# Mixing the end of layer 0 into layer 1's first projections

## The chip, the cores and the metric

The kernel runs on one core of one Trainium2 chip. A core has five engines that work at the same time and wait for one another by semaphores: PE (TensorE, matmuls, with its weight loads shown as PEld), DVE (VectorE), ACT (ScalarE), POOL (GpSimd) and SP (SyncE, which here only starts DMA transfers). Matmul results land in PSUM, which has eight banks; everything else is held in SBUF or in the chip's HBM. The metric is the device time of one execution in microseconds (us), lower is better.

## The reference

Two layers, each x + s * silu(f), where s is an attention and f a feed-forward network (FFN), both of the same layer-normalized input. The input is 4 batches of 512 tokens of 512 numbers.

```python
x  = L0_attn_x                                   # (4, 512, 512)
xn = _layernorm(x, axis=-1)
s  = _L0_attn_ref(xn, ...)    # softmax attention, 32 heads of 16, 8 key/value heads
g  = _silu(_L0_ffn_ref(xn, ...))   # Hadamard-mixed, gated: silu(x Wg) * (x Wu), then W_down
x  = x + s * g
xn = _layernorm(x, axis=-1)
s  = _L1_attn_ref(xn, ...)    # gated delta rule: q, k, v by projection, causal conv of 4, silu; 6 heads of 64
g  = _silu(_L1_ffn_ref(xn, ...))   # relu MLP with sign(weights), 512 -> 2048 -> 512
x  = x + s * g
```

In layer 1 the projections come first: q, k and v are x W, then a convolution over four time steps, then silu; a gate x Wg and two small columns (beta and the decay) are computed beside them. Then a scan over the tokens, which the kernel does in tiles of 128 tokens with a triangular solve.

## The kernel before

The program is written in program order, one helper after the other, and a scheduler at build time lays down each engine's order: it takes what is earliest in program order and, by its own estimate of durations, ready. On the chip each engine then runs its list strictly in that order and waits where an operand isn't there.

**Layer 0** is a loop over units `u`. A unit of attention is a quarter of the heads' work on 128 tokens: with 4 batches and 8 groups of heads there are `NU` = 256 units, 8 in each set of (batch, group). In unit `u` the loop emits:

- `maxima(u)`, L399 and L400: two score matmuls into the PSUM tile `sc` (one buffer of two banks), and a DVE reduction of it to the row maxima `nmx`;
- `exps(u - 11)`, L420 and L422: the transposed scores into `st` (one buffer of two banks) and exp on ACT into `pe`;
- after every eighth unit `max_rows` (L405 to L411), which folds the maxima into the queries, and, 11 units later, `values` (L430 to L452): 32 small matmuls, a copy to `os`, a round trip through HBM that turns the sums into reciprocals (`sum_d`, `rc`, `rec_d`, `sm`, with a DVE reciprocal at L440), the product on POOL (L446, `oT`) and four DMAs into `oTc`;
- two half pieces of the FFN, `ffn(v, 0)` and `ffn(v, 1)`, of the piece `v = u - 16`. A batch has 64 pieces: in the first 32 `gate_up` (L313, 4 matmuls a half, weights from `wS` by DMA, drained by ACT and DVE at L319 to L324), in the last 32 `down` (L331, 1 matmul call a half, two instructions; the PSUM tile `y` collects 16 halves and is drained at L334 and L335 into `g`).

For the batch before, `layer_sum` (L462 to L467: out projection of the attention, times `g`, POOL adds x, stored to `x1_d`) and `norm1` (L61 to L69 statistics with an ACT square root, L73, four transposes at L476, ACT copy, stored to `xn1_d`) are emitted at fixed units of the next batch. The last batch has no next one. There the loop stops at unit 269, `end_of_layer0` emits the FFN pieces 254 and 255, the four sums and the four norms, and layer 1 follows.

**Layer 1's projections** are a list of steps with weights: `projections(0)` fills `steps` with `gate1` for the last block (L741; weight 4.0), `decays`, nine times `project` (L689; 8 matmul instructions; L695 on ACT, three times L697 on DVE, L701 on ACT, L702 on DVE; weight 3.4), `to_tokens` one projection later (L713, four transposes, a square and, at L727, a DVE reduction; 0.45), two more `gate1` (3.6 each) and `norms`. The weights come by `load_wp` (L598) into three buffers of `wp`, on SP's queue between the other DMAs. PSUM for all of these is `bank()`, three buffers of one bank, which take the place of `sc` and `st` once attention has ended. Before, the steps are emitted in one go after `end_of_layer0`.

After them `l0.close()` gives back layer 0's SBUF and PSUM. Into that space go, among others, the small constants of layer 1 (L846 to L856, the loads on ACT's queue; L856 multiplies `drow` by `osc` on DVE), the copies `xsh` and `xsl` of the input (L871, L873), and the FFN of layer 1, `up1` (L913) and `down1` (L927), whose pieces are spread between the steps of what follows. The next stage, `within` (L959 to L987), begins the scan's tiles.

Of the kernel before, what the change touches and what calls it, by code (L numbers as in the profile page):

```python
# [19 lines left out]
NB, SEQ, DM = 4, 512, 512  # L20
NT = NB * SEQ // P
TB = SEQ // P
# [11 lines left out]
def kernel(ctx: ExitStack, tc: tile.TileContext, i: dict, out: bass.AP):  # L34
# [66 lines left out]
    if True:  # L101
# [164 lines left out]
        def fold_down(a):  # L266
            ph = misc()
            nc.tensor.matmul(ph, hmat, wdn[:, a, :], start=True, stop=True)
            nc.vector.scalar_tensor_tensor(wdn[:, a, :], ph, cdn[:, a : a + 1], drow, ALU.mult, ALU.mult)
# [67 lines left out]
        def ffn(u, part):  # L337
            b, r = u // 64, u % 64
            if r < 32:
                gate_up(b, r // 2, r % 2, part)  # L340
            else:
                down(b, (r - 32) // 8, 2 * (r % 8) + part)
# [7 lines left out]

        sets = [(b, g) for b in range(NB) for g in range(HG)]
        NU, LAG, LATE = 8 * len(sets), 11, 16
        qds, qTs, nmxs, qms, pes = {}, {}, {}, {}, {}

        def queries(b, v, jj):
# [123 lines left out]
        piece, zp = [0], []  # L481
# [18 lines left out]
        for n in range(FF // P):  # L500
            u = LATE + 2 * n - 4
# [3 lines left out]
        for q in range(NI):  # L505
            early.setdefault(q, []).append(lambda q=q: mix_down(q))

        for u in range(NU + LATE):
            b, r = u // 64, u % 64
            v = u - LATE  # L510
            piece[0] = max(v, 0)
            if v == 32:
                top.close()
                zp.append(l0.enter_context(tc.tile_pool(name="zp", bufs=2, side="right")))
            if 0 < u - LAG <= NU and (u - LAG) % 8 == 0:
                values((u - LAG) // 8 - 1)
            if u < NU:
                maxima(u)
            if 0 <= u - LAG < NU:
                exps(u - LAG)  # L520
            for f in early.get(u, ()):
                f()
            if v >= 0:
                ffn(v, 0)
                ffn(v, 1)
            if u % 8 == 7 and u < NU:
                max_rows(u // 8)
            if u % 32 in (22, 23) and u + 10 < NU:
                queries((u + 10) // 64, (u + 10) % 64 // 32, u % 32 - 22)
            if u % 8 == 0 and u + 8 < NU:  # L530
                set_queries(u // 8 + 1)
            if 16 <= v < 16 + NI:
                fold_down(v - 16)
            if 0 < b < NB and r in (18, 19, 20, 21):
                layer_sum(b - 1, r - 18)
            if 0 < b < NB and r in (25, 26, 28, 29):
                norm1(b - 1, (25, 26, 28, 29).index(r))
            if b + 1 < NB:
                if r == 34:
                    load_x(b + 1)  # L540
                if r in (43, 44, 45, 46):
                    stats0(b + 1, r - 43)
                if r == 49:
                    norm0(b + 1)
                if r == 52:
                    keys_values(b + 1)
            if u == NU + LAG + 2:
                break

        def end_of_layer0():  # L550
            for v in range(NU + LAG + 3 - LATE, NU):
                piece[0] = v
                ffn(v, 0)
                ffn(v, 1)
            for t in range(TB):
                layer_sum(NB - 1, t)
            for t in range(TB):
                norm1(NB - 1, t)

    att.close()  # L560

# [219 lines left out]
    steps = []  # L781
# [48 lines left out]
            add(0.0, *between.pop(0))  # L830

    projections(0)
    end_of_layer0()
    for _, f, args in steps:
        f(*args)
    steps.clear()
    l0.close()

# [475 lines left out]
    n = 0  # L1314
    for count, pinned, l in parts:
        total, done, first = sum(x[0] for x in l), 0.0, n
# [54 lines left out]
```

## Time and profile before

| | us |
|---|---|
| three runs, median (lowest, highest) | 1551.44 (1547.99, 1556.83) |
| the profiled execution | 1545.31 |
| its span, first to last instruction | 1543.5 |
| PE busy / DVE / ACT / POOL | 1452.9 / 1061.2 / 693.9 / 360.1 |
| last `maxima` (L399) starts | 761.6 |
| last `values` (L430) starts | 791.3 |
| last FFN matmul of layer 0 (L331) ends | 800.7 |
| first step of layer 1 (L741) starts | 801.6 |
| last `gate1` of the first projections (L741) ends | 875.2 |

How to read it: the page gives the busy time of each engine over the span, and the span in forty slices. A timeline row is start, length, engine, line, operation, the tiles written and read, how many instructions, and in square brackets how long the engine stood idle before the row and what ended that idle time. "x20" after a matmul row is twenty instructions back to back. Busy time of PE is that of pipelined matmuls, so the useful number is where it is not busy. A row's waiting engine isn't always to blame: the wait has a releaser, which may itself have waited.

### The profile page before, as it was taken

The numbers are of one execution on the slowest core, as the hardware profiler recorded it, in microseconds if no ns is written. First come the engines' busy times: TensorE is split into PE (matmuls) and PEld (weight loads), VectorE is DVE, ScalarE is ACT, GpSimd is POOL, SyncE is SP. The second block draws the span as 40 slices with busy tenths as digits, with TensorE's granted clock in tenths as the row PEclk, the third lists the DMA queues.
The fourth block names the chain that finished last, engine by engine and source line by source line (L and its number), as shares of the span: only waits on it lengthen the run. The fifth ranks groups of instructions, "written<-read, shape, count | busy, mean of one in ns | idle before, by whom it ended". The sixth has DMA issues, their size and how long they took to land.

```text
span 1543.5 us, 22781 instructions
## 1 busy us (share of the span) xinstructions
PE 1452.9 (94%) x8144; PEld 870.2 (56%) x8144; DVE 1061.2 (69%) x1890; ACT 693.9 (45%) x1009; POOL 360.1 (23%) x350
## 2 busy tenths in 40 slices
PE   6999999999999999999997999999999999988896
PEld 3466533555345543465343566876578756865674
DVE  6899755765566655665417679579956896588675
ACT  4654554665456654575433435224332434232132
POOL 1012100321013310222003421243204422244012
PEclk9999999999999999999998999999999999999798
DMA  8956300564026620364025343425452545224323
GB/s 281 345 184 207 139 24 22 190 226 138 25 67 211 221 84 23 120 228 143 19 80 166 94 120 104 118 83 157 132 146 55 151 125 151 70 83 145 100 79 106
DMA packets 201753, 199.14 MB, mean 129 GB/s; under 512 B 65480, under 2 KB 153000, under 8 KB 200744
## 3 DMA queue, kind: packets, MB, share of 16 engines
q1 hardware_dynamic: 198888, 196.55, 40.5%
q10 hardware_dynamic: 2752, 1.14, 0.3%
q8 instruction: 64, 1.05, 0.3%
q14 instruction: 49, 0.40, 0.1%
HBM read 146.84 MB, written 46.19 MB: 125 GB/s over the span
## 4 chain that ended last, share of the span: by engine, by line
PE 63%; DVE 23%; DMA 5%; issue 3%; POOL 2%; ACT 2%; SPq 2%; ACTq 0%; DVEq 0%; POOLq 0%
PE y L331 15%; PE mm L313 12%; PE y L927 4%; PE ph L913 4%; PE sc L399 4%; DVE UT L1022 3%; DVE sx L1018 3%; DVE yc L697 2%; PE pu L741 2%; DVE nmx L400 2%; PE mm L430 2%; PE pu L1120 2%; PE pu L1144 2%; PE pu L982 2%; PE pu L969 1%
## 5 line engine op out<-in xcount | busy, mean ns | idle before, releaser
L400 DVE TENSOR_REDUCE nmx<-sc 128x2 f32<-128x1024 f32 x256 | 312.3, 1220 | 163.5 <-PE st L420 150.4
L422 ACT ACTIVATE pe<-st 128x1024 f16<-128x1024 f32 x256 | 262.6, 1026 | 147.7 <-PE st L420 146.6
L331 PE MATMUL y<-wdn,hT 128*128 128x512 f32 x512 | 252.5, 617 | 3.2 <-DVE g L335 1.7
L313 PE MATMUL mm<-xr,wc 128*128 128x512 f32 x768 | 206.4, 410 | 0.0
L313 PEld LDWEIGHTS mm<-xr,wc 128*128 128x128 f32 x768 | 137.3, 189 | 48.6 <-issue 21.7
L324 POOL TENSOR_TENSOR hT<-hT,th 128x512 f32<-128x512 f32 x64 | 84.1, 1314 | 330.9 <-ACT hT L323 299.9
L331 PEld LDWEIGHTS y<-wdn,hT 128*128 128x128 f32 x512 | 87.1, 189 | 97.3 <-issue 89.7
L689 PE MATMUL pu<-xn1T,wp 128*128 128x512 f32 x288 | 132.9, 605 | 0.0
L898 ACT ACTIVATE sg<-sw 128x512 fp32r<-128x512 f32 x128 | 79.7, 625 | 113.8 <-issue 51.4
L913 PE MATMUL ph<-xsh,sg 128*128 128x512 f32 x256 | 114.3, 446 | 2.8 <-ACT sg L898 2.8
L399 PE MATMUL sc<-kT,qT 32*128 32x512 f16 x512 | 103.3, 384 | 6.5 <-DVE nmx L400 5.9
L446 POOL TENSOR_TENSOR oT<-os,sm 128x512 f16<-128x512 f32 x32 | 41.2, 1287 | 280.5 <-DMA sm<-rec_d 231.0
L913 PE MATMUL ph<-xsl,sg 128*128 128x512 f32 x256 | 103.5, 404 | 0.0
L420 PE MATMUL st<-qm,kT 32*128 32x512 f16 x512 | 101.4, 385 | 1.6 <-ACT pe L422 1.6
L399 PEld LDWEIGHTS <-qT 32*128 32x128 f16 x512 | 26.3, 91 | 132.4 <-issue 128.2
L927 PE MATMUL y<-sg,hsh 128*128 128x512 f32 x256 | 84.0, 439 | 9.2 <-DVE hsh L871 5.7
L918 ACT ACTIVATE hT<-ph,upsc 128x512 f32<-128x512 f32 x64 | 43.7, 683 | 102.5 <-PE ph L913 102.3
L689 PEld LDWEIGHTS pu<-xn1T,wp 128*128 128x128 f32 x288 | 54.7, 195 | 57.3 <-issue 55.8
L313 PE MATMUL mm<-xr,fo 128*128 128x512 f32 x256 | 74.1, 423 | 0.9 <-DVE fo L244 0.9
L927 PE MATMUL y<-sg,hsl 128*128 128x512 f32 x256 | 73.6, 402 | 0.0
L319 ACT ACTIVATE th<-mm,hwg 128x512 f32<-128x512 f32 x64 | 44.0, 688 | 57.7 <-PE mm L313 57.7
L1022 DVE TENSOR_TENSOR UT<-UT,sx 96x31 f32<-96x31 f32 (+31 forms) x155 | 67.2, 434 | 3.3
(285 smaller groups left out, 2426.0 us busy)
## 6 DMA issues: line engine op xcount, KB each, us to landing
wc<-wS SPq DMA_DIRECT2D x96, 512.0 KB
wS<-fo SPq DMA_DIRECT2D x16, 1024.0 KB
sw<-in_upT SPq DMA_DIRECT2D x64, 256.0 KB
sw<-in_downT SPq DMA_DIRECT2D x64, 256.0 KB
sm<-rec_d SPq DMA_DIRECT2D x128, 64.0 KB
raw<-in_w_gateT SPq DMA_DIRECT2D x8, 512.0 KB
hT<-in_w_downT SPq DMA_DIRECT2D x16, 256.0 KB
raw<-in_w_upT SPq DMA_DIRECT2D x8, 512.0 KB
```

Source lines behind the costliest of these rows:

```text
L313: nc.tensor.matmul(pgs[m], wcs[b, c, m][:, h, k, :], xrs[b][:, k, :], start=(k + h == 0), stop=(k == KC - 1 and h == 1))
L324: nc.gpsimd.tensor_tensor(hT, hT, ths[b, c], ALU.mult)
L331: nc.tensor.matmul(ys[t], hTs[b, c][:, ts(t, P)], wdn[:, c, :], start=(c == 0), stop=(c == NI - 1))
L399: nc.tensor.matmul(sc[:, j, :], qTs[n][rows, ts(t, P)], kTs[b, g // 4][rows, :], start=True, stop=True)
L400: nc.vector.tensor_reduce(nmxs[n][:, t, 2 * pr : 2 * pr + 2], sc, AX.X, ALU.max, negate=True)
L420: nc.tensor.matmul(st[:, j, :], kTs[b, g // 4][rows, ts(k, P)], qms[n][rows, :], start=True, stop=True)
L422: nc.scalar.activation(pes[u], st, AF.Exp)
L689: nc.tensor.matmul(pp, wps[b, n][:, k, 0:P], xn1Ts[b][:, k, :], start=(k == 0), stop=(k == KC - 1))
L898: tc.keep_in_program_order(nc.scalar.activation(sgs[b, c, m], raws[b, c, m], AF.Sign))
L913: ins = nc.tensor.matmul(ph, sgs[b, c, 0][:, ts(k, P)], xss[b][n][:, k, :], start=(k + n == 0), stop=(k == KC - 1 and n == 1))
L927: ins = nc.tensor.matmul(yss[b][t], hss[b, c][n][:, ts(t, P)], sgs[b, c, 1], start=(c + n == 0), stop=(c == NI - 1 and n == 1))
L1022: nc.vector.tensor_tensor(U[:, 0 : j + 1, j + 1 :], U[:, 0 : j + 1, j + 1 :], x, ALU.add)
```

## The change

Two things are changed.

In layer 0's loop, the FFN no longer runs at two half pieces a unit to the end. `halves(u)` counts the half pieces emitted before unit `u`: up to unit 212 it is 2 (u - 16) as before, from there on it grows by 3 halves in 2 units. Unit 212 is the 21st of the last batch, and the rate holds through the rest of that batch's `gate_up` and the first part of its `down`. The loop now ends with unit 267, that of the last `values`, when 476 of the 512 halves are out.

The other 36 halves, the four `layer_sum` and the four `norm1` of the last batch go into a list `rest`. The steps of `projections(0)` are then emitted as before, and after each step as many items of `rest` as keep the share of `rest` at 1.5 times the share of the steps' weight. `end_of_layer0` is gone. What each helper computes, and its tiles, stay as they are.

```diff
         sets = [(b, g) for b in range(NB) for g in range(HG)]
-        NU, LAG, LATE = 8 * len(sets), 11, 16
+        NU, LAG, LATE, SLOW = 8 * len(sets), 11, 16, 212
+
+        def halves(u):
+
+            return 2 * (min(max(u, LATE), SLOW) - LATE) + (3 * max(u - SLOW, 0) + 1) // 2
+
...
-        for u in range(NU + LATE):
+        for u in range(NU + LAG + 1):
             b, r = u // 64, u % 64
-            v = u - LATE
+            v = halves(u) // 2 if u >= LATE else u - LATE
             piece[0] = max(v, 0)
...
-            if v >= 0:
-                ffn(v, 0)
-                ffn(v, 1)
+            for h in range(halves(u), halves(u + 1)):
+                ffn(h // 2, h % 2)
...
-            if u == NU + LAG + 2:
-                break
-
-        def end_of_layer0():
-            for v in range(NU + LAG + 3 - LATE, NU):
-                piece[0] = v
-                ffn(v, 0)
-                ffn(v, 1)
-            for t in range(TB):
-                layer_sum(NB - 1, t)
-            for t in range(TB):
-                norm1(NB - 1, t)
+
+        def last_half(h):
+            piece[0] = h // 2
+            ffn(h // 2, h % 2)
+
+        rest = [(last_half, h) for h in range(halves(NU + LAG + 1), 2 * NU)]
+        rest += [(f, NB - 1, t) for f in (layer_sum, norm1) for t in range(TB)]
...
     projections(0)
-    end_of_layer0()
-    for _, f, args in steps:
+
+    total, done, n = sum(x[0] for x in steps), 0.0, 0
+    for w, f, args in steps:
         f(*args)
+        done += w
+        while n < len(rest) and n < 1.5 * len(rest) * done / total:
+            rest[n][0](*rest[n][1:])
+            n += 1
     steps.clear()
     l0.close()
```

## The prediction

> **What bounds the kernel now.** First the page: busy shares and the forty slices.
>
> ```profile
> PE 1452.9 (94%) x8144; PEld 870.2 (56%) x8144; DVE 1061.2 (69%) x1890; ACT 693.9 (45%) x1009; POOL 360.1 (23%) x350
> ...
> PE   6999999999999999999997999999999999988896
> ```
>
> TensorE is busy for 94% of the span, so moved work can gain only where it stands still. Slices are 38.6 us; the only dip inside the kernel is the 7 in the 22nd (811 to 849 us), where layer 0 hands over to layer 1. Next, the busy time by stretches there (columns: stretch, length, busy us and count of PE, weight loads, DVE, ACT, POOL, then granted clock, DMA share, GB/s).
>
> ```profile
> 800.00:810.00 10.00, 10.00 (x50) 6.58 (x49) 4.98 (x19) 2.50 (x6) 1.26 (x1) 1.00 0.37 111
> 810.00:820.00 10.00, 6.11 (x27) 3.10 (x26) 9.12 (x25) 1.44 (x3) 4.49 (x4) 1.00 0.36 118
> 820.00:830.00 10.00, 7.43 (x25) 3.50 (x24) 9.94 (x18) 5.76 (x8) 0.00 (x0) 0.83 0.53 163
> 830.00:840.00 10.00, 7.94 (x26) 3.71 (x24) 5.17 (x8) 4.97 (x9) 4.18 (x8) 1.00 0.71 199
> 840.00:850.00 10.00, 7.12 (x18) 3.79 (x19) 4.72 (x9) 2.56 (x5) 2.95 (x5) 0.66 0.53 162
> 850.00:860.00 10.00, 8.57 (x28) 4.07 (x27) 8.79 (x12) 4.88 (x8) 5.33 (x6) 1.00 0.21 61
> ```
>
> From 800 to 875, where the first projections end, PE is busy for 61.13 of 75 us: **13.87 us idle**. From 810 to 830 DVE is full instead; from 830 to 850 nothing is. The timeline tells which waits these are.
>
> ```profile
> 791.86 8.85 PE L331 MATMUL y<-wdn,hT 128*128 128x512 f32 x20
> ...
> 819.38 0.66 PE L713 MATMUL pu<-identf,yc 128*128 128x128 f32 x4 [3.52 <-DVE yc L702]
> 819.88 5.29 PE L689 MATMUL pu<-xn1T,wp 128*128 128x512 f32 x8
> 827.06 1.11 PE L476 MATMUL mm<-identf,xn 128*128 128x128 f32 x8 [1.89 <-DVE xn L73]
> ...
> 842.88 1.11 PE L713 MATMUL pu<-identf,yc 128*128 128x128 f32 x4 [4.95 <-DVE yc L702]
> 843.79 5.36 PE L689 MATMUL pu<-xn1T,wp 128*128 128x512 f32 x8
> ```
>
> The last FFN matmuls end at 800.7; from then on no filler is left. At 819 the transposes of the first projected block wait for DVE, which ran layer 0's sums and statistics first. At 843 they wait again, and DVE itself stood at one instruction:
>
> ```profile
> 841.74 0.49 DVE L856 TENSOR_SCALAR drow<-drow,osc 128x512 f32<-128x512 f32 x1 [4.13 <-DMA osc<-in_output_scale]
> ```
>
> The chain of waits names what is before it: the last store of normalized rows (2.73 us), whose end frees layer 0's memory, then 5.07 us for a load of one number. Eight projection matmuls take 3.60 us elsewhere, but 5.29 and 5.36 after these two idles, and four transposes 1.11 instead of 0.60: the slower clock cost 1.69 + 1.76 + 0.51 = **3.96 us**. With the idle, 17.8 us are lost. The smaller idles are 0.38, 1.89 and 0.68 (sums and normalization) and 0.16 + 1.26 + 1.03 = 2.45 (later projections).
>
> The Trainium skill, "TensorE: Matmul & The Clock Gate", Part 1, states that the clock falls to half once an activity window of about 3.4 us was idle and needs a busy one to recover. Here idles of 3.52 and 4.95 us were followed by mean clocks of 0.83 and 0.66, and the idles of 1.89 and less by none. By that rule a stall cut to half of 4.95 us costs no clock; were the clock's loss to shrink in proportion instead, 1.1 us of it would remain and the sum below would be 1.1 us smaller.
>
> **Part 1: attention runs ahead from unit 212.** Before, each unit carries two half pieces of FFN; after, one and a half. Before unit 267 the halves issued fall from 502 to 475, 27 fewer. No matmul is added or removed. Four down matmuls in the steady state take 1.91 us, so 27 halves are 25.8 us: the last set's value product moves from 791.3 to about 765.5, and 36 halves stay for the mix instead of the 10 in the x20 row.
>
> The cost is cover. A unit's two score pairs take 0.32 us of PE, a gate half 2.06 / 2 = 1.03, a down half 0.96. The score bank is single, and its shortest turn seen is 1.69 us:
>
> ```profile
> 719.80 0.25 DVE L440 RECIPROCAL rc<-rc 128x16 f32<-128x16 f32 x1 [1.57 <-DMA rc<-sum_d]
> 719.97 0.63 DVE L320 SCALAR_TENSOR_TENSOR th<-th,mm 128x512 f32<-128x512 f32 x1
> 720.51 1.21 DVE L400 TENSOR_REDUCE nmx<-sc 128x2 f32<-128x1024 f32 x1
> 722.20 1.22 DVE L400 TENSOR_REDUCE nmx<-sc 128x2 f32<-128x1024 f32 x1 [0.48 <-PE st L420]
> ```
>
> A unit with two halves lasts 2.38 us and hides it; one with a single half lasts 1.35 and doesn't. The mean, 1.5 x 1.03 + 0.32 + about 0.15 for the value products, is 2.0 us, above 1.69. If the built order pulls the next half forward, nothing is lost. If it keeps strictly to the program, 18 gate units lose 0.34, three down units 0.41 and six units after the last score 0.35 (exp's own turn, 48.25 to 49.88, is 1.63, against 0.32 + 0.96): 6.1 + 1.2 + 2.1 = 9.4 us. The order isn't strict: between 45 and 52 us eight gate matmuls are cut into groups of 1, 5 and 2 around attention matmuls. I take 2 us, nearest to the 724 to 768 stretch, where PE lost 0.57 of 44 us (1.3%, so 1.4 of the 110 us that 55 units of 2.0 last), and a little for the thinner cover; both ends, 0 and 9.4, stay for the range. The weight loads of the gate halves (512 KB each on SP) come no denser per PE time than before.
>
> **Part 2: 36 halves, four sums and four norms mixed into the projections.** Step weights total 46.15, and 44 items go out at 1.43 per unit of weight: six after the gate step, then about five per projection; halves end after projection 5, sums and norms after projection 6. So:
>
> - The 3.52 us wait and its 1.69 of clock go. For projections 0 to 5 DVE has 3.6 us of work each (three at 0.74, 0.69, 0.68), PE has 3.44 + 0.44 + 5 x 0.89 = 8.3 us. The transposes come after about 4.4 us of halves and a 3.4 us projection, their chain takes about 5. Saved: 5.2 us.
> - The sums and norms still come in a burst, now over projections 5 to 8: DVE has 2.6 (sums), 3.2 (statistics), 2.4 (root, four normalizations), 3.5 (L871 and L873) and three projections (10.8), 22.5 us; PE has 3.5 + 1.8 + 3 x 3.9 + 3.7 = 20.7. POOL's four adds at 1.17 pass three squares at 1.04 (L726), 7.8 us and no bound. Of 2.95 us idle, half stays. Saved: 1.5 (0 to 2.95; DVE's surplus could add 2).
> - L856 still stands in DVE's queue behind a 5.07 us load that starts when the norm store ends. What waits behind it is the conv chain of a projection. Cover is now projection 8 and two gate steps (3.4 + 3.7 + 3.8), which need little of DVE but are limited by three banks. Half of 4.95 stays; 2.5 us of idle is nearer to the 1.89 that cost no clock than to the 3.52 that did, so the 2.27 goes. Saved: 4.7 (0 to 7.2).
> - The 2.45 us of late projections stay.
>
> Saved together 11.4 us. Moved DMAs: four 256 KB stores of x1 and four of xn1 on SP, past the weight loads of projections 7 and 8; their reader is batch 3's projection, hundreds of us later, so they cost nothing unless they hold SP's queue.
>
> **New costs.** The gate step needs a 1 MB xn1T and a weight load, issued when the value product ends; before, 9.6 us of FFN and sums covered them exactly. Now the halves behind it do, if the order places enough: 0 to 4 us (the weight load waited 3.9 us on SP for wba), I take 0.5, since PE waits for no load in the listing of waits. About twenty more switches between FFN and projections cost 0 to 2 us (a first L913 behind L689 took 0.64 against 0.23), I take 0.5, as most switch between alike matmuls.
>
> The Trainium skill, same page, Part 2, "Step-by-step", says that only weight loads are pulled ahead and matmuls stay in program order. It speaks against the change: a half queued behind a waiting transpose fills nothing. Rows agree, as at 819.38 the eight matmuls queued behind ran only 0.5 us after the wait ended. By the rule any misjudged order costs its full wait, by the sum above only what the built order left uncovered.
>
> **The sum:** 11.4 - 2 - 0.5 - 0.5 = 8.4 us. The profiled execution took 1545.31 us (span 1543.5); minus 8.4 it is 1536.9, a factor of 0.9946. On the median of 1551.44 that is 1543.
>
> **Rivals.**
> 1. *Everything covered.* All 17.8 us go at 1 us of cost: 1545.31 - 16.8, on the median 1534.6. For it: FFN filler exceeds the idle twice over. Against: halves end by projection 5, before the burst and L856.
> 2. *The stalls come back.* Burst and L856 stall in full with their clock, the gain of the first wait is eaten by the burst's longer DVE queue, and 3 us of new cost remain: 0 to +3, 1553. For it: L856 isn't touched. It holds if PE idles as much after the mix as before.
> 3. *Attention's score bank becomes the bound, slower.* Units 212 to 267 run strictly in order: 9.4 us, and the seven waits for rc, which stand in DVE's queue ahead of the reductions, cost their 1.57 each, because no slack is left: 11.0. Sum 20.4 + 1 - 11.4 = +10, 1561.5. For it: single halves last less than the bank's turn. Against: the cut groups. It decides from 12 us lost there.
>
> **How the numbers follow.** Forecast 0.47 (own range 1538 to 1548), rival 1 0.15, rival 2 0.20, rival 3 0.18. About 0.5% (7.8 us, so 1543.7 and 1559.2) can be told from no change. Faster: rival 1 and 0.6 of the forecast, 0.43. Slower: most of rival 3, 0.17. Same: the rest, 0.40. The range 1534 to 1559 leaves out half of rival 1 and over half of rival 3, together under 0.2.
>
> **What would show it.** Last L399 near 742 instead of 761.6, and PE over 97% busy from 650 to 766. No L713 wait above 1 us while L331 still runs; the first L741 without a DMA wait. L856 again waiting for osc, with a PE wait under 3.4 us and no clock below 1.0. Projections ending near 866 instead of 875. Idle at L399 or L420 of 10 us and more would make the prediction wrong, as would a gap at the first gate step.

## The result, and the profile after

The changed kernel takes **1555.36 us** (median of 14 runs, 1550.98 to 1559.83) and the kernel before 1550.54 us (14 runs beside it). The ratio is 1.0037, interval 1.0021 to 1.0052: slower by 0.4%, where 0.5% faster was forecast. On a second chip the unchanged pair gave 1.0066 (1.0043 to 1.0089). The profiled execution of the changed kernel took 1559.80 us (span 1558.1), that of the kernel before 1545.31 (1543.5). These two lie 14.5 us apart and the medians 4.8, so the profiles overstate the loss; they say where it lies in one execution, the ratios how large it is.

Line numbers behind L350 are 5 or 6 higher than before: the score matmul is now L405, its reduction L406, the exp's matmul L426, the division L446, the gate step's L741 and the projection's L689 are unchanged, drow is L861, the sign L903, the first matmul of layer 1's FFN L918. In the experiments' own traces the lines stand up to 19 higher; the names of the tiles are the same.

First the page: busy shares, TensorE's forty slices and its clock.

```profile
PE 1460.6 (94%) x8144; PEld 877.1 (56%) x8144; DVE 1065.0 (68%) x1890; ACT 693.0 (44%) x1007; POOL 360.9 (23%) x350
...
PE   6999999999999999999989899999999999998796
...
PEclk9999999999999999999999999999999999999798
```

The 7 of the 22nd slice is gone, and instead the 21st (779 to 818 us) and the 23rd (857 to 896 us) show an 8. PE's busy time grew by 7.7 us with the same 8144 matmuls, for the most part by the slower clock (6.8 us in the ledger below). The busy time by stretches of 25 us shows the places (columns as before: stretch, length, busy us and count of PE, weight loads, DVE, ACT, POOL, then granted clock, DMA share, GB/s).

```profile
675.00:700.00 25.00, 22.13 (x111) 13.09 (x111) 14.81 (x18) 13.65 (x18) 5.14 (x4) 0.86 0.57 185
...
775.00:800.00 25.00, 19.99 (x79) 9.03 (x79) 1.63 (x5) 6.66 (x9) 2.48 (x7) 0.86 0.36 95
800.00:825.00 25.00, 25.00 (x75) 12.28 (x75) 13.62 (x38) 5.74 (x12) 1.27 (x1) 1.00 0.20 58
825.00:850.00 25.00, 25.00 (x67) 11.34 (x66) 10.38 (x15) 5.76 (x10) 1.04 (x1) 1.00 0.11 31
...
875.00:900.00 25.00, 19.40 (x115) 13.91 (x114) 12.30 (x17) 6.68 (x13) 18.68 (x25) 0.92 0.62 195
```

From 800 to 850, where the kernel before stood most, PE is busy for 50.00 of 50 us: the mixing does what it says. The loss is ahead of it and behind it. The ledger below cuts both traces at the same events. Idle is the time in which no matmul's record runs; the clock's loss is half the length of each window that the profile marks with half clock.

| stage, to its last event | length before, after | idle before, after | lost to clock before, after |
|---|---|---|---|
| attention: reduction of unit 208 to last exp | 155.0, 148.1 | 1.68, 9.14 | 0, 3.41 |
| handover: to the first gate matmul (L741) | 12.0, 12.5 | 0.00, 5.01 | 0, 3.14 |
| projections: to the last L689 | 61.6, 67.4 | 12.84, 0.98 | 5.12, 0.27 |
| two gate steps: to their last L741 | 11.7, 15.3 | 1.03, 2.61 | 0, 1.71 |
| next: to the next batch's first L741 | 23.6, 33.7 | 1.38, 5.23 | 0, 3.41 |
| sum | 263.9, 277.0 | 16.93, 22.97 | 5.12, 11.94 |

Idle and clock together grew by 6.04 + 6.82 = 12.86 us of the 13.1 by which the stretch grew: the ledger closes to 0.3 us, so nearly all of the loss is waiting and slower clock. Behind it both traces run alike (14.5 us apart at the first gate matmul of the next batch, 14.6 at the end). Three new waits are the largest parts of it; the timelines show them (start, duration, engine, line, operation, in brackets the idle time before and its releaser).

The first is in attention.

```profile
676.87 0.25 DVE L446 RECIPROCAL rc<-rc 128x16 f32<-128x16 f32 x1 [2.63 <-DMA rc<-sum_d]
677.04 1.16 DVE L406 TENSOR_REDUCE nmx<-sc 128x2 f32<-128x1024 f32 x1
...
678.26 0.61 PE L405 MATMUL sc<-kT,qT 32*128 32x512 f16 x2 [2.87 <-DVE nmx L406]
...
678.80 3.78 PE L313 MATMUL mm<-xr,wc 128*128 128x512 f32 x8
```

DVE stands 2.63 us at the reciprocal, whose load has not landed. The reduction behind it in the queue is late, the score bank is not free, and PE stands 2.87 us. Eight gate matmuls then take 3.78 us in place of some 2.1. It happens thrice: 2.87, 1.71 and 1.28 us, 5.86 of the stage's 9.14 us of idle.

The second is at the handover.

```profile
787.02 0.88 ACTq L609 DMA_DIRECT2D nega<-in_A_log  x1
...
791.53 0.21 ACT L617 ACTIVATE nega<-nega 128x6 f32<-128x6 f32 x1 [5.22 <-DMA dtb<-in_dt_bias]
791.65 0.58 ACT L334 ACTIVATE th<-y 128x512 f32<-128x512 f32 x1
791.77 0.17 DVE L618 TENSOR_SCALAR nega<-nega 128x6 f32<-128x6 f32 x1 [19.75 <-ACT nega L617]
...
793.00 3.78 PE L331 MATMUL y<-wdn,hT 128*128 128x512 f32 x4 [5.01 <-DVE g L335]
```

The FFN's tanh (L334) and product g (L335) are queued behind the exp and the negation of A_log, a load that starts only once attention has freed its memory. In the kernel before the same stand of DVE (13.1 us at L618) held nobody. Four down matmuls then take 3.78 us at half clock instead of 1.91.

The third is in the setup of layer 1's chunks, which starts when layer 0's last store has ended.

```profile
873.80 0.74 POOL L868 MEMSET U<- 128x768 f32 x1 [8.75 <-DMA xn_d<-xo]
...
880.43 0.77 DVE L861 TENSOR_SCALAR drow<-drow,osc 128x512 f32<-128x512 f32 x1 [4.20 <-DMA osc<-in_output_scale]
...
883.36 0.60 ACT L745 ACTIVATE cth<-pu 128x512 f32<-128x512 f32 x1 [7.48 <-DMA wrow<-in_o_norm_w]
...
884.53 0.50 PE L918 MATMUL ph<-xsh,sg 128*128 128x512 f32 x1 [3.43 <-ACT sg L903]
```

The setup's first load came 38 us later (873.7 instead of 835.7 us), and layer 1's first FFN matmul at 884.5 instead of 852.5. PE waits 3.43 us for a sign that stands behind ACT's 7.48 us. Of the three half-clock windows in these two stages (3.41 us each, from 868.8, 885.9 and 899.5 us) only the second follows this wait. The first follows waits of 0.45 and 1.75 us for normalized rows and the last projection's block, the third one of 0.95 us in the scan.

### The profile page after: what moved, and what is told of

Same layout as the page of the kernel before. It is cut to its first block, busy times and chain, and to the rows that moved or that the text cites. A ratio compares the mean times of both kernels' runs of the same rounds, so it can differ in the third digit from the quotient of the medians.

```text
span 1558.1 us, 22794 instructions
## 1 busy us (share of the span) xinstructions
PE 1460.6 (94%) x8144; PEld 877.1 (56%) x8144; DVE 1065.0 (68%) x1890; ACT 693.0 (44%) x1007; POOL 360.9 (23%) x350
## 5 line engine op out<-in xcount | busy, mean ns | idle before, releaser
L406 DVE TENSOR_REDUCE nmx<-sc 128x2 f32<-128x1024 f32 x256 | 312.3, 1220 | 154.1 <-PE st L426 139.0
L313 PE MATMUL mm<-xr,wc 128*128 128x512 f32 x768 | 211.0, 414 | 0.0
L903 ACT ACTIVATE sg<-sw 128x512 fp32r<-128x512 f32 x128 | 79.6, 625 | 113.7 <-issue 54.6
L689 PE MATMUL pu<-xn1T,wp 128*128 128x512 f32 x288 | 129.6, 592 | 0.0
L918 PE MATMUL ph<-xsh,sg 128*128 128x512 f32 x256 | 113.8, 444 | 7.6 <-ACT sg L903 7.6
L405 PE MATMUL sc<-kT,qT 32*128 32x512 f16 x512 | 104.1, 385 | 12.3 <-DVE nmx L406 11.6
L426 PE MATMUL st<-qm,kT 32*128 32x512 f16 x512 | 102.3, 386 | 1.6 <-ACT pe L428 1.6
L918 PE MATMUL ph<-xsl,sg 128*128 128x512 f32 x256 | 102.7, 401 | 0.0
L405 PEld LDWEIGHTS <-qT 32*128 32x128 f16 x512 | 27.2, 91 | 133.9 <-issue 129.3
L689 PEld LDWEIGHTS pu<-xn1T,wp 128*128 128x128 f32 x288 | 53.7, 190 | 56.9 <-issue 55.5
L1023 DVE TENSOR_TENSOR sx<-Ab,UT 96x31 f32<-96x31 f32 (+31 forms) x155 | 62.5, 403 | 5.9 <-POOL UT L1014 2.9
```

Source lines behind the costliest of these rows:

```text
L313: nc.tensor.matmul(pgs[m], wcs[b, c, m][:, h, k, :], xrs[b][:, k, :], start=(k + h == 0), stop=(k == KC - 1 and h == 1))
L405: nc.tensor.matmul(sc[:, j, :], qTs[n][rows, ts(t, P)], kTs[b, g // 4][rows, :], start=True, stop=True)
L406: nc.vector.tensor_reduce(nmxs[n][:, t, 2 * pr : 2 * pr + 2], sc, AX.X, ALU.max, negate=True)
L426: nc.tensor.matmul(st[:, j, :], kTs[b, g // 4][rows, ts(k, P)], qms[n][rows, :], start=True, stop=True)
L689: nc.tensor.matmul(pp, wps[b, n][:, k, 0:P], xn1Ts[b][:, k, :], start=(k == 0), stop=(k == KC - 1))
L918: ins = nc.tensor.matmul(ph, sgs[b, c, 0][:, ts(k, P)], xss[b][n][:, k, :], start=(k + n == 0), stop=(k == KC - 1 and n == 1))
```

## The experiments

All ratios are to the kernel before, run beside each kernel on the same chip: e1 to e4 on one chip, e5 to e8 on a second, e9 to e12 on a third, e13 to e16 on a fourth, where the kernel before had medians of 1550.86, 1547.95, 1545.91 and 1552.13 us. The same changed kernel gave 1.0037 on one chip and 1.0066 on another, so differences of some 0.003 between chips show nothing. The ratio is not exactly the quotient of the medians. Lengths in the table are of the ledger's stages, in us, in one profiled execution each.

| kernel | attention | handover | projections | gate steps | next | median us | ratio, interval |
|---|---|---|---|---|---|---|---|
| before | 155.0 | 12.0 | 61.6 | 11.7 | 23.6 | | 1 |
| e1 changed, again | 149.3 | 12.3 | 67.2 | 15.2 | 33.1 | 1562.58 | 1.0066, 1.0043 to 1.0089 |
| e2 ahead alone | 147.0 | 25.7 | 69.7 | 12.4 | 20.4 | 1562.06 | 1.0060, 1.0039 to 1.0081 |
| e3 mixing alone | 156.3 | 10.9 | 51.5 | 17.1 | 29.6 | 1550.65 | 0.9993, 0.9974 to 1.0012 |
| e4 reciprocal on GpSimd | 144.5 | 12.6 | 67.8 | 15.5 | 33.8 | 1577.24 | 1.0146, 1.0120 to 1.0172 |
| e5 A_log early | 145.7 | 9.7 | 67.2 | 13.8 | 35.5 | 1555.58 | 1.0040, 1.0022 to 1.0058 |
| e6 constants early | 145.7 | 10.2 | 70.2 | 13.8 | 33.1 | 1557.40 | 1.0064, 1.0040 to 1.0089 |
| e7 factor 4 | 146.2 | 12.3 | 77.8 | 13.6 | 21.1 | 1557.02 | 1.0057, 1.0041 to 1.0073 |
| e9 division later (not moved) | 143.8 | 12.3 | 67.1 | 13.8 | 34.0 | 1558.06 | 1.0061, 1.0038 to 1.0083 |
| e13 division pinned later | 143.3 | 12.7 | 67.2 | 15.3 | 32.7 | 1555.76 | 1.0025, 1.0003 to 1.0046 |
| e12 ahead, mended | 145.2 | 9.7 | 75.0 | 12.6 | 23.6 | 1556.69 | 1.0055, 1.0036 to 1.0074 |
| e15 ahead, mended and pinned | 144.5 | 10.2 | 75.0 | 12.6 | 23.6 | 1553.85 | 1.0010, 0.9993 to 1.0027 |
| e14 mended, from unit 240 | 149.2 | 12.0 | 67.6 | 10.2 | 23.2 | 1555.74 | 1.0021, 1.0003 to 1.0040 |
| e10 before, constants early | 156.4 | 12.0 | 57.7 | 12.5 | 21.1 | 1547.16 | 1.0000, 0.9984 to 1.0016 |
| e8 mixing, constants first | 154.7 | 13.1 | 54.6 | 13.6 | 27.7 | 1543.97 | 0.9986, 0.9969 to 1.0002 |
| e11 mixing, constants among steps | 155.5 | 10.5 | 54.2 | 11.8 | 29.3 | 1542.30 | 0.9974, 0.9956 to 0.9993 |
| e16 mixing, as e11 and pinned | 161.3 | 11.5 | 53.0 | 12.0 | 28.1 | 1544.14 | 0.9953, 0.9933 to 0.9974 |

**The two parts apart (e1, e2, e3).** The changed kernel again; then attention ahead, with all of the rest ahead of the steps; then the mixing with attention left as it was.

```diff
+    for f, *args in rest:                                      # e2
+        f(*args)
     for w, f, args in steps:
         f(*args)
-        done += w
-        while n < len(rest) and n < 1.5 * len(rest) * done / total:
-            rest[n][0](*rest[n][1:])
-            n += 1
...
-        NU, LAG, LATE, SLOW = 8 * len(sets), 11, 16, 212
+        NU, LAG, LATE, SLOW = 8 * len(sets), 11, 16, 512   # e3
```

> The changed kernel once more, for a second profile: its first profiled execution took 1559.8 us, the median of its runs 1555.4. All theories expect the median again at 1.003 to 1.005 of the kernel before. The theory that attention lost its cover expects waits for rc of 1.3 to 3 us in PE's row of score matmuls in this profile as well, and the theory that the handover got worse expects the 5 us wait for g before the first gate step and the setup of layer 1 starting near 874 us. What differs between the two profiles (a clock window of 6.8 us at half speed after the longest rc wait, above all) is chance and not the change.

> Only the first part of the change: one and a half halves a unit from unit 212, but all that is left over (36 halves, sums, norms) is emitted ahead of the projections, as before. Theory A (attention ran out of cover: PE idles 7 us more between units 212 and 267, plus clock) expects this kernel to keep that loss and to gain only the hidden round trip of the last set: 0 to +8 us against before, with the same rc waits. Theory B (the loss is in the mix: layer 1's setup starts 38 us later and is exposed in the next stage) expects it at least 4 us faster than the changed kernel, with layer 1's constants loaded before 850 us and no idle of more than 1.5 us after the projections.

> Only the second part: attention and FFN at two halves a unit to the end, so that 8 halves, four sums and four norms are left for the mix. Theory A expects the attention stretch as in the kernel before (PE idle under 2 us from 634 to 791) and the whole at or below the kernel before, 0 to -5 us. Theory B expects the late setup (constants loaded near 870 us) and with it 5 to 10 us lost after the projections, so +2 to +8 us against before.

Attention ahead alone costs what the whole change costs; the mixing alone changes nothing that can be measured. In e3 only 8 half pieces, four sums and four norms are mixed in, 16 items for 44, and the projections still shrink by 10.1 us: their idle falls from 12.84 to 4.68 us. So there was little for the other 28 half pieces to fill. In e3 the gate steps and the next stage give 11.4 us back, on the profile's lengths. Half of that is one wait of 5.46 us at the transposes before the gate steps, behind DVE's 3.64 us for osc: the late setup. e1 lies above the 1.003 to 1.005 that was expected, and e2 beyond its 0 to +8 us.

**DVE's stand at the reciprocal (e4, e9).** e4 takes the reciprocal off DVE, as a power of -1 on GpSimd. e9 issues the division and what follows it two units later.

```diff
-            nc.vector.reciprocal(rc, rc)
+            nc.gpsimd.tensor_tensor(rc, rc, neg16, ALU.pow)    # e4
...
+            if u - LAG >= 8 and (u - LAG) % 8 == 2:            # e9
+                divide((u - LAG) // 8 - 1)
```

> The changed kernel with one thing moved: the reciprocal of the softmax sums (line 446 of the changed kernel) runs on POOL, as the power -1, and no longer on DVE, so that the wait for its DMA round trip stands in POOL's queue, not ahead of the score reductions. Theory A expects the three PE waits at the score matmuls (5.9 us) and the half-clock window behind them to go: 5 to 10 us faster than the changed kernel, last exp near 775 instead of 784 us. If the thin cover itself, and not the rc wait, was the loss, the waits stay and the time changes by less than 2 us.

> The changed kernel, with the division behind each value product (reciprocal, its store, the broadcast loads, the product on GpSimd) issued two units later, so that VectorE does not stand at the reciprocal for its load. Theory (VectorE's stands at rc are what the score matmuls wait for when a unit has one half piece less, and the clock falls after the longest): the score waits fall from 5.9 us in 3 to under 1.5, no half clock near 678 us, the stretch from unit 208's reduction to the last exp takes 142 to 145 us instead of 148.1 (155.0 before the change), and the run 4 to 6 us less than the changed kernel; ratio 1.000 to 1.003. Rival (the turn of the single score bank in units with one half binds, rc or not): the waits only change their name, the stretch keeps 147 to 149 us, ratio 1.004 to 1.007.

e4 took 1577.24 us, 1.0146 (1.0120 to 1.0172): the power costs far more than the wait. The listing of tile rc in e4:

```profile
L448 POOL TENSOR_TENSOR rc<-rc,neg x32: 2898/2899/3369, 76.5 to 806.5; 128x16 f32<-128x16 f32 x32
```

2.9 us (min, median, max in ns) where DVE's reciprocal takes 0.25. But DVE was free of the stand, the score waits fell from 5.9 to 1.1 us, no half clock followed in attention, and the stretch from unit 208 to the last exp took 144.5 us. Yet PE was still idle for 6.68 us of that stretch, at exps, gate weights and drains, against 9.14 in the changed kernel and 1.68 in the kernel before: most of the idle stays when its first name is gone.

e9 does not answer its question: the order of instructions is built from estimated times, and put the reciprocal back behind reductions 221, 230, 238, 246 and 253, as in the changed kernel. Its trace has the same stand (L454 is its reciprocal), and yet a stretch of 143.8 us, since no half clock followed:

```profile
672.08 0.25 DVE L454 RECIPROCAL rc<-rc 128x16 f32<-128x16 f32 x1 [2.75 <-DMA rc<-sum_d]
672.25 1.16 DVE L406 TENSOR_REDUCE nmx<-sc 128x2 f32<-128x1024 f32 x1
673.46 0.39 PE L405 MATMUL sc<-kT,qT 32*128 32x512 f16 x2 [2.99 <-DVE nmx L406]
...
673.79 2.12 PE L313 MATMUL mm<-xr,wc 128*128 128x512 f32 x8
```

**The handover and the late setup (e5, e6, e7).** e5 loads A_log at the start and takes its exp and sign in unit 15; e6 loads the four small constants before the steps instead of behind layer 0's close; e7 mixes faster.

```diff
+            if u == LAG + 4:                                   # e5
+                nc.scalar.activation(nega, nega, AF.Exp)
+                nc.vector.tensor_scalar(nega, nega, -1.0, None, ALU.mult)
...
     projections(0)
+    upsc = new(ce, [P, NI], F32, "upsc")                       # e6; drow, osc, wrow alike
+    nc.scalar.dma_start(upsc, i["up_scale"])
...
-        while n < len(rest) and n < 1.5 * len(rest) * done / total:
+        while n < len(rest) and n < 4.0 * len(rest) * done / total:   # e7
```

> The changed kernel, with A_log loaded, exponentiated and negated during layer 0 instead of at the handover. Theory (a new wait at the handover: the sum g of gate piece 31 stands in VectorE's queue behind the negation of exp(A_log), 5.0 us, with 6.8 us of half clock after it): g's wait falls below 1 us, the clock stays at 1.0 in 785 to 800 us, the first gate step starts 4 to 6 us earlier against unit 208, and the run takes 5 to 8 us less than the changed kernel, ratio to the kernel before 0.999 to 1.002. Rival (the end is set by layer 0's last store and the setup of layer 1's chunks, which come no sooner): the first gate step moves, but the last projection and everything behind it do not; ratio 1.004 to 1.007 as without the edit.

> The changed kernel, with the four small constants of layer 1's chunks (up_scale, down_scale, output_scale, o_norm_w) loaded before the mixed steps rather than behind layer 0's close. Theory (late constants: VectorE's 4.2 us for output_scale, ScalarE's 7.5 us at 876 to 883 us and TensorE's 3.4 us for the first sign are one chain): these three waits go, the stage from the last gate copy to the next projections' last one takes 33 to 36 us instead of 39.2, and the run 3 to 6 us less than the changed kernel; ratio 1.000 to 1.003. Rival (the clears of U and T on GpSimd, which wait 8.8 us for layer 0's last store, set that stage): the waits for the constants go but the stage keeps 38 to 40 us; ratio 1.004 to 1.007.

> The changed kernel with the factor 1.5 of the mixing raised to 4.0, so that layer 0's rest is out after a quarter of the steps' weight instead of two thirds. Theory (late close): GpSimd's first clear of U comes some 15 to 25 us earlier than 873.8 us, the stage behind the last gate copy takes 30 to 35 us instead of 39.2; TensorE loses again at most 4 us in the second half of the steps; the run takes 4 to 8 us less than the changed kernel, ratio 0.999 to 1.002. Rival (the mixed work only moves: what the later stage wins, the transposes' waits in the steps lose, as in the kernel before): more than 6 us of waits at the transposes and at the first output-projection pieces after 835 us; ratio 1.003 to 1.007.

The lists of PE's waits between 660 and 930 us: the changed kernel again (e1), then e5, e6, e7, in this order (us in total, times, longest).

```profile
PE y L331 <- DVE g L335: 5.7, 2, 4.9
PE ph L918 <- ACT sg L903: 4.5, 1, 4.5
```

```profile
PE ph L919 <- ACT sg L904: 4.7, 1, 4.7
PE y L333 <- DVE g L337: 3.5, 2, 2.8
```

```profile
PE pu L741 <- DMA wp<-in_wg1T: 6.3, 1, 6.3
...
PE y L331 <- DVE g L335: 0.8, 1, 0.8
```

```profile
PE pu L713 <- DVE yc L702: 4.2, 3, 2.1
PE mm L482 <- DVE xn L73: 2.4, 2, 2.0
...
PE ph L918 <- ACT sg L903: 0.2, 1, 0.2
```

Each edit moves the wait that it aims at, and each leaves or makes another. In e5 g's wait shrinks to 2.8 us, and the first gate step starts 5.5 us earlier in the profile and stays so to the next batches. Of these, 2.8 us are the handover; 2.4 are a shorter attention stage, which the edit does not touch. Its ratio stands below e1's, but the intervals overlap and the chips differ. In e6 the sign's wait goes and g's falls to 0.8 us, but the built order now has the gate step ahead of the half pieces that had stood before it. It waits 6.3 us for weights whose load is issued 7.0 us after the last exp starts, much as in the changed kernel (7.1): nothing gained. In e7 the setup comes in time and the next stage returns to 21.1 us, but the projections take 77.8 instead of 67.4: the rival, work that only moves. None reached its theory's ratio; e6 and e7 came out at their rivals' ratios.

**The mixing with the constants out of the way (e8, e10, e11).** e8 is e3 with the edits of e5 and e6; e11 the same with the constants loaded after 0.3 of the steps' weight and scaled after 0.7; e10 the same two edits on the kernel before.

```diff
+        if part == 0 and done > 0.3 * total:
+            part = 1
+            nc.scalar.dma_start(upsc, i["up_scale"])
...
+        if part == 1 and done > 0.7 * total:
+            part = 2
+            nc.vector.tensor_scalar(drow, drow, osc, None, ALU.mult)
```

> The mixing alone (attention not ahead: 8 halves, sums and norms among the steps), with A_log's part and the four small constants early as in the two edits before. Theory (the mixing wins some 10 us at the last projection, and the late close and constants take them back in the next stage): the win at the last gate copy (4.9 us with the mixing alone) grows to 6 to 10 us and stays to the end; ratio 0.993 to 0.997. Rival (the clears, key and value tiles and signs of the next stage bind whatever the constants do): the end moves by less than 2 us against the mixing alone; ratio 0.998 to 1.001.

> The kernel before, untouched in its order, with exp(A_log) early and the four small constants of layer 1's chunks loaded among the steps rather than behind layer 0's close. Theory (the wait of drow for output_scale cost TensorE 4.95 us and 2.27 us of clock, as the prediction priced it): the second wait of the transposes, at 843 us, falls below 1 us with full clock, and the run takes 5 to 7 us less, ratio 0.995 to 0.997. Rival (what follows the close, the clears and the last norms, fills the same gap): 0.999 to 1.001.

> The mixing alone (8 half pieces, sums and norms among the steps, attention not ahead) with the same early constants as the control on the kernel before, loaded among the steps. Theory (mixing and early constants remove different idles, the first transposes' wait and the drow wait): 3 to 6 us less than that control, ratio 0.992 to 0.995. Rival (they fill the same gap, the control has all the gain): within 2 us of the control.

In e10 the transposes' wait for drow at 843 us is gone (3.17 us at 826, then 0.95, 0.71 and 0.42), and the profile is 4.2 us shorter from unit 208 to the next batch's gate step; yet the runs show no gain (1.0000, its rival's range), so of the 7.2 us that I had priced for drow and its clock nothing measurable comes back by itself. e8 came out as its rival too (0.9986, with an interval that reaches 1). e11 gains (0.9974, the interval below 1), though its ratio is nearer to 1 than expected; its median is 4.9 us below e10's on the same chip. So the mixing and the early constants together give a gain clear of 1, and neither does alone; since e11's interval overlaps those of e3, e8 and e10, more than this is not shown.

**Attention ahead with everything mended (e12, e13, e14, e15, e16).** e12 is the changed kernel with e5's edit, e11's constants, the factor 2.5 and the division two units later (which again left the reciprocal behind the same reductions); e14 is the same with attention ahead from unit 240. In e13 (the changed kernel), e15 (as e12) and e16 (as e11) the reciprocal is held in the program's order, three units behind:

```diff
+            tc.keep_in_program_order(nc.vector.reciprocal(rc, rc))
...
+            if u - LAG >= 8 and (u - LAG) % 8 == 3:
+                divide((u - LAG) // 8 - 1)
```

> The changed kernel with all that was found late mended: the division two units later, exp(A_log) early, the four constants among the steps, the mixing's factor 2.5. Theory (attention ahead loses only by what it uncovers; mended, it is worth what it brings, which is little beside the mixing alone, since 16 mixed items already fill the idle): within 3 us of the mixing alone with early constants, ratio 0.993 to 0.998. Rival (attention ahead itself is the loss, through units whose single half is shorter than the turn of the score bank): 5 us or more above the mixing alone with early constants, ratio 0.999 to 1.003.

> The changed kernel with the reciprocal held three units behind its value product, in VectorE's queue behind the reductions of those units (in the earlier run with the later division the builder of the order put it back where it had been: behind reductions 221, 230, 238, 246 and 253, as in the changed kernel). Theory (VectorE's stands at rc are the score matmuls' waits and, through them, the half clock at 678 us): the score waits fall from 5.2 to 5.9 us to under 2, the stretch from unit 208's reduction to the last exp takes 141 to 144 us, and the run is at 1.001 to 1.004. Rival (thin units lose the time anyway, in other waits): stretch 144 to 149, ratio 1.005 to 1.007.

> The mended kernel (exp(A_log) early, constants among the steps, factor 2.5) with attention ahead only from unit 240, so that 14 half pieces are moved instead of 28. Theory (each moved half saves less in attention than it costs in the steps, where 16 mixed items have already filled the idle; the loss grows with the halves moved): midway between the mixing alone with early constants (0.9974) and the mended kernel (1.0055), so 1.000 to 1.003. Rival (the loss is one event, the starved reciprocal and half clock near 675 us, before unit 240): 0.996 to 0.999.

> The mended kernel with attention ahead from unit 212 and the reciprocal held three units behind. Theory (rc's stands are a part, some 4 us, of the loss against the mixing alone; the rest is that the idle in the steps was already filled): 1.001 to 1.004. Rival (they are all of it): 0.996 to 0.999; rival (none of it): 1.005 to 1.007.

> The mixing alone with early constants and the reciprocal held three units behind. With two halves in a unit the stands of VectorE at rc cost TensorE under 1 us, so the pinning should change nothing: 0.995 to 0.999, as without it (0.9974). A ratio above 1.001 would say that the pinning itself costs (later normalized rows for the layer sums).

The waits of e13 (list of PE's waits, 620 to 930 us):

```profile
PE sc L405 <- DVE nmx L406: 4.1, 5, 1.2
...
PE st L426 <- ACT pe L428: 1.4, 1, 1.4
```

The longest score wait is 1.2 us instead of 2.9, and no half clock follows in attention. But the waits did not go below 2 us in sum, as the theory had it; they came in smaller pieces. The traces show how little the pin moved. For the stage of attention (us; the reductions that stand in DVE's queue ahead of the five reciprocals between 670 and 765 us, and how long DVE stands at these five):

| kernel | reductions ahead | DVE's stands | PE's score waits | PE idle | lost to clock | length |
|---|---|---|---|---|---|---|
| before | 221, 230, 238, 245, 253 | 2.71 | 0.36 | 1.68 | 0 | 155.0 |
| e11 mixing, constants | 221, 230, 238, 245, 253 | 2.43 | 0.78 | 2.15 | 0 | 155.5 |
| changed | 221, 230, 238, 246, 253 | 7.96 | 5.86 | 9.14 | 3.41 | 148.1 |
| e9 not moved | 221, 230, 238, 246, 253 | 7.14 | 5.25 | 7.56 | 0 | 143.8 |
| e13 pinned | 222, 230, 238, 246, 254 | 5.83 | 4.05 | 6.85 | 0 | 143.3 |
| e12 not moved | 221, 230, 238, 246, 253 | 6.36 | 4.50 | 7.52 | 1.71 | 145.2 |
| e15 pinned | 222, 230, 238, 246, 254 | 5.53 | 3.74 | 7.77 | 0 | 144.5 |

The pin holds the reciprocal back by one reduction in two of the five sets; in the other three the built order already had it there. Attention becomes 0.5 us shorter from e9 to e13 and 0.7 from e12 to e15, and its idle hardly changes.

In the runs the ratio falls from e12 to e15 from 1.0055 to 1.0010, with intervals that don't meet, and from e9 to e13 by 0.0036. But each of these pairs lies on two chips, and from e11 to e16, where the reciprocal cost little, it falls by 0.0021 as well. The profiles of e12 and e15 end 7.0 us apart, and over the five stages they differ by 0.2; 4.1 of the 7.0 lie between the first gate steps of the next two batches. So what the pinning is worth is not shown. e13 and e15 have ratios in their theories' ranges and e16 the one expected, but the traces don't bear out the theory that the stand at the reciprocal is what attention loses by.

e15 against e16, on one chip: 1.0010 (0.9993 to 1.0027) against 0.9953 (0.9933 to 0.9974). With all that was found mended, attention ahead still costs 0.57%, some 9 us; e12 against e11, on another chip, shows 0.8%, more than e12's theory and its rival expected. Both kernels that run ahead also mix at 2.5 instead of 1.5, which was not tried apart. **e16 beats both kernels**: 1544.14 us beside 1552.13 of the kernel before.

e14's ratio lies where "each moved half costs" put it, but its trace does not support that: up to the next batch's gate step it is only 0.8 us longer than e11 (262.2 against 261.4, sums of the table's row). Then it loses 7.4 us to e11 by the gate step of the batch after, 5.0 of them near 990 us, where e11 has no wait:

```profile
990.21 0.50 PE L937 MATMUL ph<-xsh,sg 128*128 128x512 f32 x1 [1.63 <-ACT sg L922]
...
995.00:1000.00 5.00, 5.00 (x20) 4.42 (x19) 1.01 (x3) 1.02 (x2) 0.83 (x1) 0.51 0.41 117
```

A sign is late by 1.63 us and 6.8 us of half clock follow. e12 and e13 have the same wait (1.15 and 1.17 us) and the same clock; e15 the wait (1.2 us) without the clock; the changed kernel itself neither. Why the mended orders meet it was not tried.

## Why the prediction was wrong

The forecast's sum was 11.4 - 2 - 0.5 - 0.5 = 8.4 us gained. The ledger of the two profiles, term by term (us, a gain is positive; the profiles lie 14.5 us apart, so its sum is larger than the loss of the medians):

| term of the sum | forecast | measured |
|---|---|---|
| attention's cover | -2 | 9.14 + 3.41 - 1.68 = -10.9 |
| the first gate step | -0.5 | 5.01 + 3.14 = -8.2 |
| first transposes' wait, burst, late constants: in the projections | +11.4 in all | 17.96 - 1.25 = +16.7 |
| the same, in the two gate steps and the next stage | | 12.96 - 2.41 = -10.6 |
| switches | -0.5 | within the ledger's rest, 0.2 |
| sum | +8.4 | -12.9 |

**The step that failed is the cover in part 1:** "I take 2 us, nearest to the 724 to 768 stretch, where PE lost 0.57 of 44 us". That stretch has two down halves in every unit, which is just the cover that the change takes away. The term measured 10.9 us in this pair. It is not one unlucky trace: in all eleven traces with attention ahead from unit 212 the idle of this stage is 6.7 to 9.3 us (1.68 in the kernel before, at most 3.0 in e3, e8, e10 and e11; 4.95 in e16, 3.25 of it for weights), and the clock's loss 0 to 5.1 us, which is partly chance. e2 and e3, on one chip, show in the runs that it is this part that costs. Within blocks of eight units the thin gate units run as hoped where nothing is late (17.3 us for 47 gate matmuls in units 224 to 232, with 0.13 us of idle, against 20.7 for 64), but the three blocks that hold a late rc had 1.42 to 2.87 us of idle. The moved work left 45 down matmuls fewer before the last exp, at 0.43 us start to start 19.3 us, and attention shortened by 6.9. The value product of the last set ran at 785.2, not 765.5, and PE was busy 92.7% from 650 to 775 us (98.7 before), not over 97%.

- **Rival 3 had the place, and the waits by name**: waits for rc in DVE's queue ahead of the reductions, "because no slack is left". In the changed kernel they are PE's longest waits in attention. That they are the cause is not shown: with the reciprocal off DVE (e4) PE's score waits fell to 1.1 us and 6.68 us of idle stayed, and the pinned kernels keep 6.85 and 7.77. The thin units lose the time in other waits as well. Its price of 20.4 us was too high: idle and clock together took 12.55 us (13.6 in e1), just past the 12 from which it was to decide. Its forecast of 1561.5 us stands near the profiled 1559.8, but 6 us above the median.
- **The first gate step** was put on its own loads. No DMA wait came there, as predicted; the wait of 5.01 us stands just ahead of it, at the half pieces. It was for g, behind ACT's and DVE's instructions on A_log. I had looked at what stands behind the moved loads, not at what the FFN's remaining pieces would now stand behind: setup code that had been harmless. With A_log early (e5) g's wait fell to 2.8 us. The prediction had named a gap at the first gate step as a sign that it would be wrong.
- **The mixing** was right in mechanism and undersized: no transpose waited over 1 us while halves ran, and the projections shed 16.7 us of idle and clock, where 11.4 were forecast in all. Part of that is the clock: by its windows the kernel before lost 5.12 us to it there, where I had read 3.96 off three groups of rows. e3 shows that 16 items suffice for most of it. That is the second thing the sum missed: it never asked how much filler the idle needed, and so whether attention had to run ahead at all. The projections of the changed kernel have 0.98 us of idle and are 5.8 us longer than before.
- **The late constants** were said to keep half of 4.95 us, with full clock. L861 did wait for osc (4.20 us), but what PE waited for was the sign (3.43 us), behind ACT's wait for wrow, and a half-clock window of 3.41 us followed. The close of layer 0 comes 38 us later, which the sum had not moved anything by. e7 shows that an earlier close removes that wait and brings back others.
- That an idle of 2.5 us costs no clock, read off 1.89 and 3.52 us, did not hold: 2.87 us, and 2.46 in e16, were followed by 6.8 us of half clock.
- Projections and gate steps were to end near 866 instead of 875; the last gate matmul started at 879.3 (874.9 before).

What stays open: by which of the thin units' waits attention loses its time, and how the 9 us between e15 and e16 divide. In the profile of e15 the five stages hold 17.5 us of idle and 3.4 of clock; attention has 7.77 us of it (2.15 in e11), so thin units go on losing, in score waits up to 1.1 us, a wait of 1.8 us for an exp and one of 0.8 for a weight load. These were not taken away one by one, nor was the wait near 990 us. The profile of e16 fell on a late weight load of 2.46 us in attention, which is why its stage is long in the table while its runs are the fastest.

## To carry to other kernels

Work that fills an engine is worth moving only until the idle at the other end is filled: count the idle there first, and ask what the work covered where it stood. When units are made shorter, small instructions that wait for a load in a queue, ahead of the one that frees the critical buffer, begin to cost: DVE's stands of 2.71 us cost 0.36 us of score waits in the kernel before, its 7.96 us cost 5.86 in the changed one. But judge a mend by the idle of the whole stage and not by the wait that had the name: here the named wait shrank and most of the idle stayed. And look in the trace whether the edit moved the instruction at all, since an order built from estimated times may put it back. Where two edits each only move a wait, try them together: here the mixing and the early constants gained 0.3% as a pair (0.5% in the run with the reciprocal pinned) and nothing measurable alone.

## What the runs showed of the hardware

How much clock an idle costs is not set by its length alone. The idle of 2.87 us in the changed kernel was followed by 6.8 us of half clock; 2.99 us in e9, at the same instruction, by none (eight gate matmuls in 2.12 us). In e16 an idle of 2.46 us, a late weight load, was followed by 6.8 us:

```profile
692.61 3.78 PE L315 MATMUL mm<-xr,wc 128*128 128x512 f32 x8 [2.46 <-DMA wc<-wS]
```

The windows of half clock around the change were 3.4 or 6.8 us long in every trace, one or two times the same length. The Trainium skill, "TensorE: Matmul & The Clock Gate", Part 1, gives that length for its activity window, calls the window free-running and has the clock fall after a whole idle one. The lengths agree. A free-running window also fits the unlike ends of like idles: in each of the 18 traces the half-clock windows start on one grid of 3.413 us to 0.003 us. On that grid 2.27 of the changed kernel's 2.87 us fall into one cell of the grid, the one before its half clock; e9's 2.99 us are cut into 1.53 and 1.46 by a cell's end. But a whole idle window was not needed: 2.46 and 2.87 us are shorter than one. Nor do the traces give a threshold of idle time: cells with 1.93 us (e5, from 783.8) and 1.96 us (e16, from 862.7) had full clock behind them, a cell with 0.54 us (e14, from 989.7) half clock.
